# Edge weights kept in FP32 through the building of a dense graph: one FP32 one-hot product per slot in place of three BF16 products

## The chip, the core and the metric

The kernel runs on one core of a Trainium2 chip. The metric is device time in microseconds (us). Three runs of the kernel before took 4602.34, 4610.16 and 4604.41 us; the median is 4604.41.

The core has five engines that run side by side, each through its own list of instructions in order: TensorE (PE in the profile; its weight loads are PEld), VectorE (DVE), ScalarE (ACT), GpSimd (POOL) and SyncE (SP, which starts DMAs). SBUF is the on-chip memory of 128 partitions, PSUM the memory that TensorE writes its products to.

## The reference, cut to what matters

A graph of 3125 nodes (features of width 128) and 100,000 edges, sorted by target, goes through four layers, each of which normalises its input and adds its result to x. The change lies in how edges become matrices. Layer 0 (attention) and layer 2 need, for each pair of target and source node, how many edges join them. Layer 1 needs the sum of the edge weights of each pair:

```python
def spmv(v):
    return jax.ops.segment_sum(edge_vals[:, None] * v[edge_col], edge_row, num_segments=n)
...
edge_index = jnp.stack([src, dst])
h = jnp.maximum(_layernorm(x, axis=-1), 0.0)
x = x + _L0_gnn_ref(h, edge_index, ...)
h = jnp.maximum(_layernorm(x, axis=-1), 0.0)
x = x + _L1_gnn_ref(h, edge_weight, L1_gnn_weights, src, dst)
```

With the two dense matrices in hand, every sum over edges is a plain matrix product: counts (how many edges) is kept in SBUF as 8-bit floats, weights (the sum of edge weights) goes to device memory in FP32 and is read back in layer 1.

## The kernel before, in words

Nodes are cut into 25 blocks of 128 (NB). The edges of one target block and one source block go to a fixed number of slots of 128 edges each: CAP[db] slots for every source block, 8 for target block 0, 4, 3, 3 for the next three, 2 for blocks 4 to 18 and 1 for blocks 19 to 24. N_SLOTS is the number of slots of a target block, made even: 200, 100, 76, 76, then 50 and 26; 1358 in all, of which 1350 are used.

**Placing (place_edges, L924).** Edges lie in a tile of 112 rows by 896. VectorE works out the place of each edge in the table (the result is idx, L1056). Each edge has a record of 8 BF16 fields (FIELDS): its source within the block (SL), its target within the block (DL), three BF16 parts of its weight (WT to WT+2) and its type (TYPE). The three parts come from split3 (L913, called at L1060): ScalarE rounds the weight to BF16, VectorE subtracts, ScalarE rounds the rest, VectorE subtracts again; the three add up to the FP32 value. For each field TensorE turns the tile (L1074) and ScalarE writes it into rec (L1075), where neighbouring edges of one field lie 16 bytes apart. Then GpSimd issues 782 scatters (L1081), each of which writes 128 rows of 32 BF16 elements (ROOM, 64 bytes) to the table in device memory. ORDER puts the edges of target block 5 and up first, those of blocks 0 to 4 last.

**Building (build_block, L1137).** One call for each target block. SyncE loads the block's records into slots (L1151), once the scatters that hold its edges have landed. TensorE turns each field so that the 128 edges of a slot lie along the partitions (L1157); the result, keys, stays in PSUM, with one buffer. Then the slots go in batches of 8 (BATCH), of which there are 187. For each batch VectorE makes two one-hot matrices, oh_s and oh_d (L1174), which hold a 1 where the edge's source or target equals the column, and three products of oh_s with a part of the weight (L1176), together called oh_w. All are BF16 and lie in pairs of slots, so that the value of slot 2a+1 is next to that of slot 2a. For each slot TensorE adds one product of oh_s and oh_d to the counts (L1188) and three products of oh_d with the parts of oh_w to the weights (L1191). Both sums of two source blocks share one PSUM tile, ps_cw, with two buffers. When a pair is complete, ScalarE writes the counts to SBUF (L1195) and the weights to w_out (L1196), and after every second pair issues a DMA of w_out (L1199). At a block's end ScalarE checks in one instruction over 3200 elements that no count is above 15 (L1201, junk). The one-hots have two buffers each (b_hot).

**What sets the order.** GROUPS lists the target blocks: 5 to 8, 9 to 12, 13 to 16, 17 to 20, 21 to 24, then 0 to 2 and 3 to 4. Each group is built and then goes through the first attention (attend, L1318): 25 products u for each block (L1331, TensorE), then for each of 4 heads and 25 source blocks one masked count matrix on VectorE (over, L1340) and up to four products on TensorE (L1343). A scheduler sets the order of each engine's list before the run, by the order of the program and by when it reckons each instruction to be ready: so u products of a block stand between the slot products of the same group. After the last group come the second attention (to about 1840 us), layer 1, which reads the weights matrix three times, layer 2 and layer 3.

Of the kernel before, what the change touches and what calls it, by code (L numbers as in the profile page):

```python
# [18 lines left out]
P = 128  # L19
N = 3125  # L20
NB = 25
# [41 lines left out]
BATCH = 8  # L63
SL, DL, WT, TYPE = 0, 1, 2, 5
CB = [(q, min(4, NB - q)) for q in range(0, NB, 4)]


def bc(ap, shape):
    return ap.to_broadcast(shape)
# [829 lines left out]
class FastGnn(Gnn):  # L899
# [24 lines left out]
    def place_edges(self, placed):  # L924


        nc, tc, a = self.nc, self.tc, self.a
        self.table = self.dram.tile([TABLE, ROOM], BF16, name="table")
        self.types = self.dram.tile([1, EPART * EC], BF16, name="types")
# [4 lines left out]
        with ExitStack() as s:  # L934
# [6 lines left out]

            rec = placed.tile([P, EK * A * FIELDS + ROOM - FIELDS], BF16, name="rec")
            rec_of = rec[:, : EK * A * FIELDS].rearrange("p (k a f) -> p k a f", k=EK, f=FIELDS)
# [5 lines left out]
            for name, dt, fill, skip, queue in loads:  # L949
# [4 lines left out]
                queue.dma_start(t[whole:, : rest - skip], v[whole * EC + skip :][None, :])  # L954
            nc.gpsimd.memset(rec, 0.0)
            per = BASE[NB] // P
            none = work.tile([P, 14 * ROOM], BF16, name="none")
            nc.gpsimd.memset(none, -1.0)
            nc.sync.dma_start(self.table[: BASE[NB]].rearrange("(p i r) f -> p i (r f)", p=P, r=14),
                              bc(none[:, None, :], [P, per // 14, 14 * ROOM]))  # L960
            number = tile("number")
# [96 lines left out]
            w = raw["edge_weight"]  # L1058
            parts = [tile(f"w16_{i}", BF16) for i in range(3)]
            self.split3(parts, w, tile("rest"), V)  # L1060
            of_i = tile("of_i", I32)
            fields = [(WT + i, p) for i, p in enumerate(parts)]
            for f, name in ((SL, "src"), (DL, "dst")):
# [55 lines left out]
    def open_build(self, s, counts):  # L1119
# [13 lines left out]
        nc.vector.memset(self.minus_most, -MOST)  # L1133
        self.above = one.tile([P, NB], F32, name="above")
        self.junk = one.tile([P, NB, P], FP8, name="junk")

    def build_block(self, db):  # L1137
# [8 lines left out]

        keys = self.b_keys.tile([P, WT + 3, N_SLOTS[0]], BF16, name="keys")
        at = sum(N_SLOTS[:db])
        for a in range(halves):
            r = self.b_slots.tile([P, P, ROOM], BF16, name="slots")  # L1150
            ld = nc.sync.dma_start(r[:rows], self.table[BASE[db] + a * rows * P :][: rows * P].rearrange(  # L1151
                "(s e) f -> s e f", e=P))
# [13 lines left out]
        for x0 in range(0, n_slots, BATCH):  # L1166
            k = min(BATCH, n_slots - x0)
            h = k // 2
            wide = [P, h, P, 2]
            key = lambda f: bc(keys[:, f, x0 : x0 + 2 * h].rearrange("p (a b) -> p a b", b=2)[:, :, None, :], wide)  # L1170
            oh_s, oh_d = (self.b_hot.tile([P, BATCH // 2, P, 2], BF16, name=m) for m in ("oh_s", "oh_d"))
            oh_w = self.b_hot.tile([P, 3, BATCH // 2, P, 2], BF16, name="oh_w")
            for oh, f in ((oh_s, SL), (oh_d, DL)):
                nc.vector.tensor_tensor(oh[:, :h], bc(lane[:, None], wide), key(f), op=OP.is_equal)  # L1174
            for t in range(3):
                nc.vector.tensor_tensor(oh_w[:, t, :h], oh_s[:, :h], key(WT + t), op=OP.mult)  # L1176
            for x in range(k):
# [6 lines left out]
                if c == 0 and sb % 4 == 0:  # L1184
# [4 lines left out]
                                 skip_group_check=True)  # L1189
                for t in range(3):  # L1190
                    nc.tensor.matmul(ps[:, 1, j, :], lhsT=oh_d[of], rhs=oh_w[:, t][of], start=False,  # L1191
                                     stop=(last and t == 2), skip_group_check=True)
                if last and (j == 1 or sb == NB - 1):
# [7 lines left out]
        nc.scalar.activation(self.junk, self.counts[:, :, db * P : (db + 1) * P], AF.Relu, bias=self.minus_most,  # L1201
                             accum_out=self.above[:, db : db + 1], saturate=False)

# [690 lines left out]
```

## Time and profile before

| what | us |
|---|---|
| median of three runs | 4604.41 |
| the profiled execution's own time | 3488.11 |
| its span, first to last instruction | 3486.2 |
| first scatter of the placing starts | 139.63 |
| building and first attention, in turns | about 230 to 1325 |
| VectorE busy in all | 2391.4 (69%) |
| ScalarE busy in all | 663.7 (19%) |
| GpSimd scatters L1081 | 763.4, 782 of 976 ns |
| oh_s and oh_d, L1174 | 118.3 and 118.1 |
| oh_w, L1176 | 324.9, 561 of 631 ns |
| counts and weights products, L1188 and L1191 | 300.8 and 387.0 |
| drains, L1195 and L1196 | 122.7 and 117.5 |

The profiled execution is shorter than the median of the plain runs by 1116.3 us. The profile covers the profiled execution alone, and no view of it shows where the difference lies.

In a row of the profile the engine and the operation are followed by what is written and what is read, the shapes, and the number of instructions; then the busy time in us and the mean of one in ns; then the idle time just ahead of them and what ended it. In a timeline the first number is the start in us, the second how long the merged instructions took. Matmul records of TensorE overlap: the step from one start to the next tells the rate, not the length of one.

### The profile page before, as it was taken

Reading aid. Unit: us, or ns where it says so; the run is one execution under the profiler, and the core shown is the slowest. Engines: PE = TensorE matmul, PEld = TensorE weight load, DVE = VectorE, ACT = ScalarE, POOL = GpSimd, SP = SyncE. Lnnn points to the kernel's source line nnn. Section 1 sums busy time; section 2 is a strip of 40 time slices with the busy share of each in tenths; the row PEclk is TensorE's granted clock in tenths of the full one; section 3 lists DMA queues with packets and bytes.
Section 4 is the critical chain, followed back from the end, with each engine's and each line's share of the span. In section 5 each row is a group of like instructions: output and inputs, shape, how many; then the busy total and the mean of one; then the engine's idle time right before and its main releaser. Section 6 shows DMA issues by size and latency. Waiting matters only on the chain. (4 is left out here: it accounts for less than half of the span.)

```text
span 3486.2 us, 50781 instructions
## 1 busy us (share of the span) xinstructions
PE 2646.8 (76%) x20474; PEld 1841.3 (53%) x20474; DVE 2391.4 (69%) x3938; ACT 663.7 (19%) x1418; POOL 1286.3 (37%) x1305
## 2 busy tenths in 40 slices
PE   0146787878777887888885989796999957778886
PEld 0034465655556554555553444345555547777785
DVE  7976999999899998999994010214555565555665
ACT  1243041322501122000001000002021022222222
POOL 1377777777777000000000000001121017777775
PEclk9978999999999998999997999897999968999998
DMA  5012131211311110000003867660000033443432
GB/s 171 16 40 67 27 96 31 79 44 56 108 23 44 37 39 19 1 1 1 1 1 135 304 227 279 242 228 13 1 1 1 1 98 106 121 114 108 130 113 56
DMA packets 117351, 277.07 MB, mean 79 GB/s; under 512 B 28037, under 2 KB 67412, under 8 KB 106148
## 3 DMA queue, kind: packets, MB, share of 16 engines
q1 hardware_dynamic: 50566, 194.31, 16.3%
q0 software_dynamic: 40128, 37.42, 4.9%
q10 hardware_dynamic: 26412, 42.00, 3.4%
q8 instruction: 163, 2.67, 0.3%
q14 instruction: 82, 0.67, 0.1%
HBM read 210.66 MB, written 62.96 MB: 78 GB/s over the span
## 5 line engine op out<-in xcount | busy, mean ns | idle before, releaser
L1081 POOL DMA_INDIRECT table<-rec,idx x782 | 763.4, 976 | 368.1 <-issue 238.1
L1343 PE MATMUL ps_acc<-parts,over 128*128 128x198 bf16 x5000 | 622.7, 253 | 163.8 <-DVE over L1340 79.2
L1343 PEld LDWEIGHTS <-over 128*128 128x128 bf16 x5000 | 375.6, 98 | 407.8 <-DVE over L1340 384.2
L919 POOL TENSOR_TENSOR rest<-z,l_parts 128x640 f32<-128x640 f32 x15 | 21.0, 1400 | 1407.1 <-ACT l_parts L918 1407.1
L1778 POOL DMA_INDIRECT m_far<-pre,src_of x472 | 461.3, 977 | 193.4 <-issue 119.8
L1340 DVE SCALAR_TENSOR_TENSOR over<-ps_row,minus,counts 128x512 bf16<-128x512 f32 (+2 forms) x700 | 424.7, 685 | 9.2 <-PE ps_acc L1343 7.1
L1191 PE MATMUL ps_cw<-oh_w,oh_d 128*128 128x128 bf16 x4050 | 387.0, 225 | 53.3 <-DVE oh_w L1176 49.1
L531 PE MATMUL ps_sum<-g,v_node 128*128 128x512 f32 (+1 forms) x1050 | 403.7, 547 | 2.2 <-ACT v_node L482 2.2
L1340 DVE SCALAR_TENSOR_TENSOR over<-row,minus,counts 128x640 bf16<-128x640 f32 x500 | 401.9, 877 | 0.6 <-ACT row L1439 0.6
L1191 PEld LDWEIGHTS <-oh_d 128*128 128x128 bf16 x4050 | 306.0, 100 | 93.3 <-issue 71.8
L1188 PE MATMUL ps_cw<-oh_d,oh_s 128*128 128x128 bf16 x1350 | 300.8, 226 | 46.9 <-ACT w_out L1196 27.4
L1176 DVE TENSOR_TENSOR oh_w<-oh_s,keys 128x1024 bf16<-128x1024 bf16 (+2 forms) x561 | 324.9, 631 | 0.0
L1600 PE MATMUL ps_agg<-l_parts,counts 128*128 128x384 bf16 (+1 forms) x1875 | 313.6, 327 | 8.7 <-POOL l_parts L921 8.7
L531 PEld LDWEIGHTS ps_sum<-g,v_node 128*128 128x128 f32 x1050 | 188.0, 190 | 218.0 <-issue 215.2
L1483 DVE COPY v<-ps_sum 128x3200 f32<-128x3200 f32 x3 | 10.5, 3492 | 404.3 <-PE ps_sum L531 404.3
L1600 PEld LDWEIGHTS <-counts 128*128 128x128 fp8e4 x1875 | 183.2, 98 | 134.9 <-issue 9.6
L1799 PE MATMUL agg_far<-m_far,oh_far 128*128 128x128 f32 x1438 | 217.8, 303 | 47.7 <-ACT m_far L1785 43.4
L1799 PEld LDWEIGHTS agg_far<-m_far,oh_far 128*128 128x128 f32 x1438 | 195.9, 213 | 55.6 <-ACT m_far L1785 54.7
L1784 DVE TENSOR_TENSOR m_far<-ps_t,m_far 128x512 f32<-128x512 f32 x118 | 81.0, 688 | 165.9 <-DMA m_far<-pre,src_of 109.7
L1195 ACT ACTIVATE counts<-ps_cw 128x256 fp8e4<-128x256 f32 (+1 forms) x325 | 122.7, 378 | 333.4 <-PE ps_cw L1191 321.2
L1796 DVE TENSOR_TENSOR oh_far<-lane,keys 128x512 f32<-128x512 f32 (+3 forms) x194 | 124.1, 642 | 71.2 <-PE agg_far L1799 70.5
L1188 PEld LDWEIGHTS <-oh_s 128*128 128x128 bf16 x1350 | 134.4, 100 | 72.7 <-issue 46.3
(348 smaller groups left out, 3376.0 us busy)
## 6 DMA issues: line engine op xcount, KB each, us to landing
g<-weights SPq DMA_DIRECT2D x75, 1600.0 KB
weights<-w_out ACTq DMA_DIRECT2D x150, 256.0 KB
src_row<-wide SPq DMA_DIRECT2D x26, 512.0 KB
table<-rec,idx POOLq DMA_INDIRECT x782
type_row<-types SPq DMA_DIRECT2D x29, 384.0 KB
table<-none SPq DMA_DIRECT2D x1, 10864.0 KB
type_row<-wide SPq DMA_DIRECT2D x26, 384.0 KB
m_far<-pre,src_of POOLq DMA_INDIRECT x472
```

The lines of the kernel that those rows point to most:

```text
L531: nc.tensor.matmul(ps[:, c, :w], lhsT=y[:, b, :], rhs=flat[:, c0 : c0 + w], start=(b == 0), stop=(b == NB - 1))
L1081: st = nc.gpsimd.indirect_dma_start(out=self.table, out_offset=bass.IndirectOffsetOnAxis(ap=idx[:, k, p : p + 1], axis=0), in_=rec[:, (k * ...
L1176: nc.vector.tensor_tensor(oh_w[:, t, :h], oh_s[:, :h], key(WT + t), op=OP.mult)
L1188: nc.tensor.matmul(ps[:, 0, j, :], lhsT=oh_s[of], rhs=oh_d[of], start=(j == c == 0), stop=last, skip_group_check=True)
L1191: nc.tensor.matmul(ps[:, 1, j, :], lhsT=oh_d[of], rhs=oh_w[:, t][of], start=False, stop=(last and t == 2), skip_group_check=True)
L1195: nc.scalar.copy(self.counts[:, q : q + n, db * P : (db + 1) * P], ps[:, 0, :n], saturate=True)
L1340: V.scalar_tensor_tensor(over[:, : n * P], row, minus[:, sb, i : i + 1], self.counts[:, sb, cols], op0=OP.is_gt, op1=OP.mult)
L1343: nc.tensor.matmul(ps[:, j, : 3 * F2], lhsT=over[:, j * P : (j + 1) * P], rhs=parts[:, sb, i].rearrange("p s f -> p (s f)"), start=(sb == ...
L1600: nc.tensor.matmul(ps[:, :n], lhsT=self.counts[:, sb, db * P : (db + 1) * P], rhs=parts[:, sb, :n], start=(sb == 0), stop=(sb == NB - 1))
L1778: nc.gpsimd.indirect_dma_start(out=m[:, j, :], out_offset=None, in_=pre, in_offset=bass.IndirectOffsetOnAxis(ap=src_of[:, a + j : a + j + ...
L1796: V.tensor_tensor(oh[:, :r], bc(self.lane[:, None, :], [P, r, P]), bc(of[d][:, lo - LOW[d] : hi - LOW[d], None], [P, r, P]), op=OP.is_equal)
L1799: nc.tensor.matmul(agg[d], lhsT=oh[:, c - lo, :], rhs=m[:, c - a, :], start=(c == LOW[d]), stop=(c == ENDS[d] - 1))
```

## The change

The weight of an edge is kept as one FP32 word in its record, in the place of its first two BF16 parts; TYPE moves from field 5 to field 4. The record tile and the table become 32-bit words of the same number of bytes, and each scatter writes 16 words, 64 bytes as before. split3 is gone from the placing; the FP32 weights are turned by TensorE in two pieces and written into the records by ScalarE. In build_block, TensorE turns two BF16 fields and the FP32 weight. VectorE makes oh_s and oh_d as before and one FP32 product oh_w in place of three BF16 ones; ScalarE copies oh_d to FP32 (oh_d32). Both FP32 one-hots are written slot by slot, through a view in pairs. TensorE adds one FP32 product for each slot to the weights in place of three BF16 ones. The check of the counts is made in five pieces of 640 elements.

```diff
-SL, DL, WT, TYPE = 0, 1, 2, 5
+SL, DL, WT, TYPE = 0, 1, 2, 4
...
-        self.table = self.dram.tile([TABLE, ROOM], BF16, name="table")
+        self.table = self.dram.tile([TABLE, ROOM // 2], I32, name="table")
...
-            rec = placed.tile([P, EK * A * FIELDS + ROOM - FIELDS], BF16, name="rec")
+            words = placed.tile([P, (EK * A * FIELDS + ROOM - FIELDS) // 2], I32, name="rec")
+            rec = words.bitcast(BF16)
+            rec_w = words[:, : EK * A * FIELDS // 2].bitcast(F32).rearrange("p (k a f) -> p k a f", k=EK, f=FIELDS // 2)
...
-            nc.gpsimd.memset(rec, 0.0)
+            nc.gpsimd.memset(words, 0)
...
-            parts = [tile(f"w16_{i}", BF16) for i in range(3)]
-            self.split3(parts, w, tile("rest"), V)
+            for q, n in ((0, 4), (4, EK - 4)):
+                ps = psum2.tile([P, 4, A], F32, name="ps_idx")
+                for j in range(n):
+                    nc.tensor.transpose(ps[:, j, :], w[:, (q + j) * P : (q + j + 1) * P], self.ident[:A, :A])
+                nc.scalar.copy(rec_w[:, q : q + n, :, WT // 2], ps[:, :n])
             of_i = tile("of_i", I32)
-            fields = [(WT + i, p) for i, p in enumerate(parts)]
+            fields = []
...
-                    in_=rec[:, (k * A + p) * FIELDS :][:, :ROOM], in_offset=None)
+                    in_=words[:, (k * A + p) * FIELDS // 2 :][:, : ROOM // 2], in_offset=None)
...
-        self.junk = one.tile([P, NB, P], FP8, name="junk")
+        self.junk = one.tile([P, 5, P], FP8, name="junk")
...
-        keys = self.b_keys.tile([P, WT + 3, N_SLOTS[0]], BF16, name="keys")
+        both = self.b_keys.tile([P, 2, N_SLOTS[0]], F32, name="keys")
+        keys = both[:, 0].bitcast(BF16).rearrange("p (f x) -> p f x", f=2)
+        w_of = both[:, 1]
...
-            for f in range(WT + 3):
-                nc.tensor.transpose(keys[:, f, a * rows : (a + 1) * rows], r[:rows, :, f], self.ident16[:rows, :rows])
+            part = slice(a * rows, (a + 1) * rows)
+            for f in (SL, DL):
+                nc.tensor.transpose(keys[:, f, part], r[:rows, :, f], self.ident16[:rows, :rows])
+            nc.tensor.transpose(w_of[:, part], whole.bitcast(F32)[:rows, :, WT // 2], self.ident[:rows, :rows])
...
-            oh_w = self.b_hot.tile([P, 3, BATCH // 2, P, 2], BF16, name="oh_w")
+            oh_w, oh_d32 = (self.b_hot.tile([P, BATCH, P], F32, name=m) for m in ("oh_w", "oh_d32"))
+            paired = lambda t: t.rearrange("p (a b) n -> p a n b", b=2)[:, :h]
             for oh, f in ((oh_s, SL), (oh_d, DL)):
-                nc.vector.tensor_tensor(oh[:, :h], bc(lane[:, None], wide), key(f), op=OP.is_equal)
-            for t in range(3):
-                nc.vector.tensor_tensor(oh_w[:, t, :h], oh_s[:, :h], key(WT + t), op=OP.mult)
+                nc.vector.tensor_tensor(oh[:, :h], bc(lane[:, None], wide), key(keys[:, f]), op=OP.is_equal)
+            nc.vector.tensor_tensor(paired(oh_w), oh_s[:, :h], key(w_of), op=OP.mult)
+            nc.scalar.copy(paired(oh_d32), oh_d[:, :h])
...
-                for t in range(3):
-                    nc.tensor.matmul(ps[:, 1, j, :], lhsT=oh_d[of], rhs=oh_w[:, t][of], start=False,
-                                     stop=(last and t == 2), skip_group_check=True)
+                nc.tensor.matmul(ps[:, 1, j, :], lhsT=oh_d32[:, x, :], rhs=oh_w[:, x, :], start=False, stop=last,
+                                 skip_group_check=True)
...
-        nc.scalar.activation(self.junk, self.counts[:, :, db * P : (db + 1) * P], AF.Relu, bias=self.minus_most,
-                             accum_out=self.above[:, db : db + 1], saturate=False)
+        for q in range(0, NB, 5):
+            nc.scalar.activation(self.junk, self.counts[:, q : q + 5, db * P : (db + 1) * P], AF.Relu, bias=self.minus_most,
+                                 accum_out=self.above[:, db * 5 + q // 5 : db * 5 + q // 5 + 1], saturate=False)
```

More of the change, by code (lines that the diff above doesn't have):

```diff
@@ L959, in place_edges @@
             nc.sync.dma_start(self.table[: BASE[NB]].rearrange("(p i r) f -> p i (r f)", p=P, r=14),
-                              bc(none[:, None, :], [P, per // 14, 14 * ROOM]))
+                              bc(none.bitcast(I32)[:, None, :], [P, per // 14, 14 * ROOM // 2]))
             number = tile("number")
@@ L1133, in open_build @@
         nc.vector.memset(self.minus_most, -MOST)
-        self.above = one.tile([P, NB], F32, name="above")
-        self.junk = one.tile([P, NB, P], FP8, name="junk")
+        self.above = one.tile([P, NB * 5], F32, name="above")
+        self.junk = one.tile([P, 5, P], FP8, name="junk")
     def build_block(self, db):
@@ L1144, in build_block @@
         need = [self.placed[c] for c in range(LOW[db], ENDS[db])]
-        keys = self.b_keys.tile([P, WT + 3, N_SLOTS[0]], BF16, name="keys")
+        both = self.b_keys.tile([P, 2, N_SLOTS[0]], F32, name="keys")
+        keys = both[:, 0].bitcast(BF16).rearrange("p (f x) -> p f x", f=2)
+        w_of = both[:, 1]
         at = sum(N_SLOTS[:db])
         for a in range(halves):
-            r = self.b_slots.tile([P, P, ROOM], BF16, name="slots")
-            ld = nc.sync.dma_start(r[:rows], self.table[BASE[db] + a * rows * P :][: rows * P].rearrange(
+            whole = self.b_slots.tile([P, P, ROOM // 2], I32, name="slots")
+            r = whole.rearrange("p e f -> p (e f)").bitcast(BF16).rearrange("p (e f) -> p e f", f=ROOM)
+            ld = nc.sync.dma_start(whole[:rows], self.table[BASE[db] + a * rows * P :][: rows * P].rearrange(
                 "(s e) f -> s e f", e=P))
@@ L1169, in build_block @@
             wide = [P, h, P, 2]
-            key = lambda f: bc(keys[:, f, x0 : x0 + 2 * h].rearrange("p (a b) -> p a b", b=2)[:, :, None, :], wide)
+            key = lambda v: bc(v[:, x0 : x0 + 2 * h].rearrange("p (a b) -> p a b", b=2)[:, :, None, :], wide)
             oh_s, oh_d = (self.b_hot.tile([P, BATCH // 2, P, 2], BF16, name=m) for m in ("oh_s", "oh_d"))
-            oh_w = self.b_hot.tile([P, 3, BATCH // 2, P, 2], BF16, name="oh_w")
+            oh_w, oh_d32 = (self.b_hot.tile([P, BATCH, P], F32, name=m) for m in ("oh_w", "oh_d32"))
+            paired = lambda t: t.rearrange("p (a b) n -> p a n b", b=2)[:, :h]
             for oh, f in ((oh_s, SL), (oh_d, DL)):
-                nc.vector.tensor_tensor(oh[:, :h], bc(lane[:, None], wide), key(f), op=OP.is_equal)
-            for t in range(3):
-                nc.vector.tensor_tensor(oh_w[:, t, :h], oh_s[:, :h], key(WT + t), op=OP.mult)
+                nc.vector.tensor_tensor(oh[:, :h], bc(lane[:, None], wide), key(keys[:, f]), op=OP.is_equal)
+            nc.vector.tensor_tensor(paired(oh_w), oh_s[:, :h], key(w_of), op=OP.mult)
+            nc.scalar.copy(paired(oh_d32), oh_d[:, :h])
             for x in range(k):
```

## The prediction, made before the changed kernel ran

> **What bounds the kernel now.** I read the page's slices first, then busy time by windows, then the groups by line, and last the timeline of single engines inside one block. Only two stages hold lines that the change touches: the placing of the edges (0 to 140 us) and the building of the blocks (230 to 1285 us), which alternates with the attention of each group.
>
> ```profile
> DVE  7976999999899998999994010214555565555665
> ACT  1243041322501122000001000002021022222222
> ...
> 400.00:500.00 100.00, 82.62 (x934) 62.67 (x935) 95.61 (x168) 38.96 (x100) 76.20 (x79) 0.97 0.26 77
> 1000.00:1100.00 100.00, 73.89 (x911) 59.18 (x910) 95.05 (x159) 12.81 (x33) 76.22 (x79) 0.93 0.11 28
> ```
>
> Slices 4 to 16 (87 us each) show VectorE at 9 and ScalarE at 1 to 3. The windows (PE, PEld, DVE, ACT, POOL busy, clock) say the same of two building stretches: VectorE 95%, ScalarE 13 to 39%, clock 0.93 to 0.97. So VectorE paces the builds.
>
> ```profile
> L1191 PE MATMUL ps_cw<-oh_w,oh_d 128*128 128x128 bf16 x4050 | 387.0, 225 | 53.3 <-DVE oh_w L1176 49.1
> L1176 DVE TENSOR_TENSOR oh_w<-oh_s,keys 128x1024 bf16<-128x1024 bf16 (+2 forms) x561 | 324.9, 631 | 0.0
> L1331 PE MATMUL ps_u<-parts,counts 128*128 128x396 bf16 x625 | 149.3, 354 | 9.2 <-ACT counts L1195 7.9 <-DVE u L1333 0.4
> L1201 ACT ACTIVATE junk<-counts,minus_most 128x3200 fp8e4<-128x3200 fp8e4 x25 | 74.1, 2966 | 0.0
> L1749 DVE TENSOR_TENSOR oh_wide<-lane,keys 128x512 f32<-128x512 f32 (+1 forms) x113 | 76.6, 678 | 18.1 <-PE agg_wide L1761 17.7 <-ACT keys L1735 0.3
> L1075 ACT COPY rec<-ps_rec 128x784 bf16<-128x784 bf16 x6 | 21.4, 3823 | 0.0
> ```
>
> TensorE's weight products wait for VectorE's oh_w, and oh_w waits for nothing (0.0). L1749 and L1075 are my prices for an FP32 VectorE product and for a strided ScalarE write.
>
> ```profile
> 256.24 0.68 DVE L1174 TENSOR_TENSOR oh_s<-lane,keys 128x1024 bf16<-128x1024 bf16 x1
> 256.83 0.68 DVE L1174 TENSOR_TENSOR oh_d<-lane,keys 128x1024 bf16<-128x1024 bf16 x1
> 257.43 1.88 DVE L1176 TENSOR_TENSOR oh_w<-oh_s,keys 128x1024 bf16<-128x1024 bf16 x3
> 259.23 0.68 DVE L1174 TENSOR_TENSOR oh_s<-lane,keys 128x1024 bf16<-128x1024 bf16 x1
> ...
> 430.54 0.22 PE L1188 MATMUL ps_cw<-oh_d,oh_s 128*128 128x128 bf16 x1
> 430.59 0.33 PE L1191 MATMUL ps_cw<-oh_w,oh_d 128*128 128x128 bf16 x3
> 430.77 0.22 PE L1188 MATMUL ps_cw<-oh_d,oh_s 128*128 128x128 bf16 x1
> ...
> 3186.43 0.22 PE L1756 MATMUL ps_m<-type,type_hot 96*128 96x128 bf16 x1
> 3186.43 0.97 PEld L1799 LDWEIGHTS agg_far<-m_far,oh_far 128*128 128x128 f32 x8
> 3186.49 1.11 PE L1799 MATMUL agg_far<-m_far,oh_far 128*128 128x128 f32 x8
> ...
> 128.12 10.65 ACT L1075 COPY rec<-ps_rec 128x784 bf16<-128x784 bf16 x3
> 138.58 1.59 ACT L1114 CAST in_order<-ps_idx 128x448 int32<-128x448 f32 x2
> ```
>
> A batch of 8 slots takes VectorE 2.99 us (256.24 to 259.23), that is 5 steps of 0.598. TensorE needs 0.228 us for a slot's four BF16 products (430.54 to 430.77), 1.82 us a batch. An FP32 product leaves two records: L1799 has 1438 records for 719 products. Eight such records follow one BF16 product; a record is 0.275 us long (median of L1799), so the last starts at 3187.33, eight steps of 0.112 us after the BF16 start at 3186.43. The BF16 product's own step is thus also 0.112, not 0.057: the FP32 weight load behind it is longer.
>
> **The skill.** "TensorE: Matmul & The Clock Gate", Weight-path perf modes, says that the fast weight load brings nothing for FP32; the 0.112 us step agrees. "VectorE: DVE Perf Modes", the perf-mode tier table, gives tensor_tensor twice the rate in BF16 only; 631 ns for 1024 BF16 elements against 678 for 512 FP32 agree. "ScalarE: Activation LUTs", What ACT_TABLE_LOAD costs, gives 186 ns plus 0.833 ns an element. "SBUF — State Buffer", Specifications, says that each move to another 16-byte line pays a penalty, without a price. L1075 writes 2-byte elements 16 bytes apart at 4.9 ns each (3823/784), L1114 FP32-sized ones 28 bytes apart at about 2.0 (1.59 us for 784), so the trace agrees.
>
> **The change part by part.** The sum is made against the profiled execution: 3488.11 us, its span of 3486.2 and 1.9 around it. The median of the runs is 1116.3 us above that, and no view shows where; I carry this part over unchanged.
>
> Placing: split3 loses two VectorE instructions of 1.07 us and two casts beside it; three rec copies of 3.6 us go, and two FP32 ones come, which need only the loaded weights and can run in ScalarE's idle time from 45 to 117 us. Now the rec copies end at 138.8 us and the first scatter starts at 139.6. Then idx, ready at 137.9 now and 2.1 earlier, is what is late. Gain 3.5 us (between 0 and 5). The scatters keep their number and 64-byte rows. Memset, fill and loads lie in the wait for inputs or move the same bytes: nothing.
>
> VectorE: per batch two one-hots at 0.598 and one FP32 product. From L1749, 0.678 plus 512 more elements at 0.96 GHz gives 1.21 us long, a step of 1.13. The batch is 2.33 in place of 2.99. Over 1358/8 = 170 full batches that frees 112 us, if nothing else binds. The product writes FP32 to places 512 bytes apart in turn; no VectorE row shows such a write. Floor 1.13, ceiling 2.2 (two cycles an element); I take the floor, since the copy below is the longer of the two either way.
>
> TensorE: a slot becomes one BF16 product and two FP32 passes in alternation, 3 x 0.111 = 0.333 us; 2.66 a batch. The u products (L1331) run in the same stage: 25 per block at 0.17 us, 0.68 a batch of a 50-slot block. So 3.34, above VectorE's old 2.99. A block's key transposes drop from five to three: under 0.3 us a block, nothing.
>
> ScalarE: the drains of a pair (L1195, L1196) take 0.61 us back to back, 1.3 a batch with the DMA issue. The new copy reads 1024 elements and writes FP32 alternately to two places 512 bytes apart. Floor 1.04 us (the ScalarE page's formula), ceiling 5.0 (L1075's 4.9 ns); I take 1.9, near L1114, the nearest write of the same width. The check of counts in five pieces costs 3.9 us a block for 2.97. ScalarE is thus 3.8 us busy per batch of a 50-slot block.
>
> The new wait: the FP32 product waits for the copy; behind it on TensorE stand all later slots and u, and VectorE waits for them to free its buffers. Each one-hot has two buffers and PSUM two pairs, so batch n+1 follows the end of batch n-1 by two one-hots (1.25), the copy (1.9), the drain that frees PSUM (0.65), then its own 3.34: 7.14 for two, 3.57 a batch. A 50-slot block takes 6.25 x 3.57 = 22.3, plus 2.1 at its start (keys 0.4, first product 3.2 late, 1.5 filled by u): 24.4 for the 20.8 measured between the starts of blocks at 444.8 and 465.6 us. Twelve such blocks are not held by scatters: +43. Six blocks of 26 slots: ScalarE's 8.6 drains, 3.9 check and 6.3 copies make 18.8 for 14.0 or less: +4.5 each, +27. Four wide blocks: (1.25 + 1.9 + 2.83)/2 = 3.0 a batch, as now, +4 at starts. With the placing: 43 + 27 + 4 - 3.5 = +70.5. The attention stages between, the second attention and layers 1 to 3 don't change. Profile 3559, median 4675.
>
> **The rivals.** A, not slower: VectorE's saving reaches the end. If the copy costs at most 1.05 us and the u products slip into the attention stage, where VectorE paces, a batch needs TensorE's 2.66: 0.33 x 170 = 56 us less, 4548. For it: VectorE's 95% and ScalarE's idle 60%. Against: u runs between the products today. It decides from the point at which a batch falls below 2.99.
>
> B: the copy is cheap, TensorE binds with u inside. 50-slot blocks +1.3 x 12, small ones +2 x 6 (ScalarE's check and drains), wide ones -0.16 x 56, placing -3.5: +15, 4619. For it: the formula; against: L1114.
>
> C: ScalarE serves the drains of batch n before the copy for n+1, or the copy costs near 5 us. Serialised, a batch is 3.34 + 0.65 + 1.9 less the hidden counts, 5.5: 2.5 x 75, plus 34 for small and 115 for wide blocks: +337, 4941. For it: the drains stand earlier in the program; against: u at 427.88 shows that the order follows readiness, and the copy is ready first.
>
> **How the numbers follow.** Forecast 0.47, its own range 4630 to 4735 (copy 1.3 to 2.7 us). A 0.18, B 0.22, C 0.13. B straddles: 0.02 faster, 0.09 within 0.2% (about what a measurement can tell from none), 0.11 slower. Faster 0.20, same 0.09, slower 0.71. From 4530 to 4760 holds the forecast, B and most of A; C and the lowest of A, under 0.2, stay out. If the 1116 us is a slower TensorE, the loss grows; if it is slower scatters, they hold the builds and it shrinks.
>
> **What would show it.** The copy's mean (1.9), block starts 24 us apart in place of 20.8, TensorE 0.333 a slot, VectorE idle in builds behind TensorE, first scatter near 136 us. A copy near 1.05 with VectorE still above 90% would prove the forecast wrong.

## The result and the profile after

The changed kernel takes 4734.68 us (median of 4 runs, 4733.06 to 4742.38), the kernel before 4607.28 in the runs beside it. The ratio is 1.0276, with a 95% interval from 1.0254 to 1.0299: slower, by some 127 us.

The first profile of the kernel before took 3488.11 us, which none of its plain runs did (4584 to 4635 us in all). A second profile of the same kernel (the first run of the experiments) took 4613.69 us, like the plain runs. The two profiles compared from here on are that one and the profile of the changed kernel (4734.26 us, span 4732.5). First the page of the changed kernel: the slices of VectorE and ScalarE (118 us each), then groups.

```profile
DVE  8502000000488788797889998011145463444545
ACT  0101000000434634646420001000021111121222
...
L1201 PE MATMUL ps_cw<-oh_w,oh_d 128*128 128x128 f32 x2700 | 538.8, 331 | 113.1 <-ACT oh_d L1187 89.2
...
L1187 ACT CAST oh_d<-oh_d 128x1024 f32<-128x1024 bf16 (+2 forms) x187 | 337.6, 1845 | 395.6 <-DVE oh_d L1185 393.8
...
L1186 DVE TENSOR_TENSOR oh_w<-oh_s,keys 128x1024 f32<-128x1024 bf16 (+2 forms) x187 | 335.8, 1796 | 50.2 <-remote 50.2
```

The same slices (115 us each) and the old products on the page of the second profile of before:

```profile
DVE  8502000000299999999899993101345563344444
ACT  0201000000113322211300001000011121122221
...
L1191 PE MATMUL ps_cw<-oh_w,oh_d 128*128 128x128 bf16 x4050 | 398.5, 227 | 95.8 <-DVE oh_w L1176 50.6
...
L1176 DVE TENSOR_TENSOR oh_w<-oh_s,keys 128x1024 bf16<-128x1024 bf16 (+2 forms) x561 | 324.8, 630 | 0.0
```

Three things are to be seen. In both of these profiles VectorE does next to nothing in slices 5 to 10: the builds run only after the last scatter (its end is at 1206.1 us before, 1204.7 after). By the end of the second attention (2780.1 us, against 1840.8 in the first profile) this makes 939 of the 1116 us that the first profile lacked; the rest lies in the layers behind it. Then, in the builds, VectorE falls from 9s to mostly 7s and 8s, and ScalarE rises from between 1 and 3 to between 3 and 6. And the oh_w products cost VectorE 335.8 us, more than the 324.8 of the three BF16 ones that they replace.

The windows show who paces now. The columns are the stretch and its length in us, busy time and instructions of PE, PEld, DVE, ACT and POOL, then PE's clock, DMA share and GB/s. In the second profile of before: a piece of the scatters, then the stretch between two attentions that builds blocks 10 to 12.

```profile
900.00:1140.00 240.00, 13.47 (x84) 8.52 (x84) 7.24 (x15) 6.08 (x12) 184.19 (x172) 0.50 0.05 10
...
1385.00:1447.00 62.00, 53.37 (x669) 42.62 (x669) 59.17 (x110) 33.27 (x84) 0.00 (x0) 1.00 0.30 101
```

The same two stretches of the changed kernel:

```profile
900.00:1140.00 240.00, 21.02 (x85) 15.34 (x85) 13.47 (x13) 12.46 (x23) 184.40 (x172) 0.50 0.05 10
...
1395.00:1487.00 92.00, 78.38 (x580) 65.62 (x580) 65.50 (x76) 74.02 (x140) 0.00 (x0) 0.93 0.20 71
```

Those three blocks took 62 us with VectorE busy 95% of it; now they take 92 with TensorE at 85%, ScalarE at 80% and VectorE at 71%. No engine is full: they hand work to each other and wait. One wait, in ScalarE's timeline of the changed kernel (start, length in us):

```profile
1587.42 0.83 ACT L1212 ACTIVATE junk<-counts,minus_most 128x640 fp8e4<-128x640 fp8e4 x1
...
1588.37 0.83 ACT L1212 ACTIVATE junk<-counts,minus_most 128x640 fp8e4<-128x640 fp8e4 x1
...
1589.20 3.76 ACT L1187 CAST oh_d<-oh_d 128x1024 f32<-128x1024 bf16 x2
...
1596.92 0.38 ACT L1205 ACTIVATE counts<-ps_cw 128x256 fp8e4<-128x256 f32 x1 [0.99 <-PE ps_cw L1201]
1597.20 0.37 ACT L1206 COPY w_out<-ps_cw 128x256 f32<-128x256 f32 x1
1597.45 2.02 ACT L1187 CAST oh_d<-oh_d 128x1024 f32<-128x1024 bf16 x1
```

VectorE's timeline of the same kernel says when those copies could have begun:

```profile
1586.52 0.68 DVE L1185 TENSOR_TENSOR oh_d<-lane,keys 128x1024 bf16<-128x1024 bf16 x1
...
1595.36 0.68 DVE L1185 TENSOR_TENSOR oh_d<-lane,keys 128x1024 bf16<-128x1024 bf16 x1
```

And TensorE's timeline what it costs:

```profile
1588.12 0.22 PE L1199 MATMUL ps_cw<-oh_d,oh_s 128*128 128x128 bf16 x1
1591.21 0.49 PE L1201 MATMUL ps_cw<-oh_w,oh_d 128*128 128x128 f32 x2 [2.87 <-ACT oh_d L1187]
...
1593.12 0.31 PE L1199 MATMUL ps_cw<-oh_d,oh_s 128*128 128x128 bf16 x1
...
1593.76 0.31 PE L1199 MATMUL ps_cw<-oh_d,oh_s 128*128 128x128 bf16 x1
```

The oh_d that ends at 1587.20 is copied from 1589.20 on: ScalarE first finishes pieces of the check of the block before. The oh_d that ends at 1596.04 is copied from 1597.45 on: in ScalarE's list the drain of the batch ahead stands first, and it waits for TensorE. From the end of an oh_d to the start of its copy it is 1.50 us in the mean (123 copies between 1230 and 2100 us). TensorE waits 2.87 us for the first copy, and soon after takes 0.64 us a slot (1593.12 to 1593.76) in place of 0.333. The windows around it show the granted clock of TensorE, the third number from the end:

```profile
1591.20:1592.35 1.15, 1.14 (x10) 1.11 (x11) 1.15 (x2) 1.15 (x1) 0.00 (x0) 1.00 0.00 0
1592.35:1595.75 3.40, 3.40 (x19) 3.09 (x18) 1.07 (x3) 1.70 (x5) 0.00 (x0) 0.50 0.02 5
1595.77:1600.00 4.23, 3.86 (x32) 3.11 (x31) 4.18 (x5) 3.24 (x7) 0.00 (x0) 1.00 0.17 64
```

The slots of 0.64 us are those at half clock. Between the last scatter and the last product of the builds TensorE is busy at half clock for 113 us in the changed kernel and for 49 us in the second profile of before.

### The profile page after: what moved, and what is told of

Same layout as the page of the kernel before. It is cut to its first block, busy times and chain, and to the rows that moved or that the text cites. A ratio compares the mean times of both kernels' runs of the same rounds, so it can differ in the third digit from the quotient of the medians.

```text
span 4732.5 us, 48211 instructions
## 1 busy us (share of the span) xinstructions
PE 2862.1 (60%) x19058; PEld 2033.6 (43%) x19058; DVE 2403.3 (51%) x3562; ACT 994.4 (21%) x1802; POOL 1340.9 (28%) x1305
## 5 line engine op out<-in xcount | busy, mean ns | idle before, releaser
L1086 POOL DMA_INDIRECT table<-rec,idx x782 | 816.8, 1045 | 380.8 <-issue 250.6
L1201 PE MATMUL ps_cw<-oh_w,oh_d 128*128 128x128 f32 x2700 | 538.8, 331 | 113.1 <-ACT oh_d L1187 89.2
L1199 PE MATMUL ps_cw<-oh_d,oh_s 128*128 128x128 bf16 x1350 | 315.6, 235 | 475.9 <-remote 310.2
L1201 PEld LDWEIGHTS ps_cw<-oh_w,oh_d 128*128 128x128 f32 x2700 | 461.0, 216 | 181.9 <-ACT oh_d L1187 119.6
L1185 DVE TENSOR_TENSOR oh_s<-lane,keys 128x1024 bf16<-128x1024 bf16 (+2 forms) x187 | 118.7, 635 | 796.8 <-remote 648.9
L1187 ACT CAST oh_d<-oh_d 128x1024 f32<-128x1024 bf16 (+2 forms) x187 | 337.6, 1845 | 395.6 <-DVE oh_d L1185 393.8
L1186 DVE TENSOR_TENSOR oh_w<-oh_s,keys 128x1024 f32<-128x1024 bf16 (+2 forms) x187 | 335.8, 1796 | 50.2 <-remote 50.2
L1342 PE MATMUL ps_u<-parts,counts 128*128 128x396 bf16 x625 | 165.2, 362 | 191.8 <-remote 109.4
L1772 PE MATMUL agg_wide<-m_wide,oh_wide 128*128 128x128 f32 x900 | 157.6, 329 | 163.4 <-ACT m_wide L1769 123.6
L1342 PEld LDWEIGHTS <-counts 128*128 128x128 fp8e4 x1250 | 120.5, 101 | 290.7 <-issue 168.7
```

The lines of the kernel that those rows point to most:

```text
L1086: st = nc.gpsimd.indirect_dma_start(out=self.table, out_offset=bass.IndirectOffsetOnAxis(ap=idx[:, k, p : p + 1], axis=0), in_=words[:, (k ...
L1186: nc.vector.tensor_tensor(paired(oh_w), oh_s[:, :h], key(w_of), op=OP.mult)
L1187: nc.scalar.copy(paired(oh_d32), oh_d[:, :h])
L1199: nc.tensor.matmul(ps[:, 0, j, :], lhsT=oh_s[of], rhs=oh_d[of], start=(j == c == 0), stop=last, skip_group_check=True)
L1201: nc.tensor.matmul(ps[:, 1, j, :], lhsT=oh_d32[:, x, :], rhs=oh_w[:, x, :], start=False, stop=last, skip_group_check=True)
L1342: nc.tensor.matmul(wide[:, : HEADS * 3 * F1], lhsT=self.counts[:, sb, (a + q) * P : (a + q + 1) * P], rhs=parts[:, sb, :, :, F1:], start=( ...
```

## The experiments

Ratios are to runs of the kernel before on the same chip (medians 4614.96, 4601.48 and 4609.35 us in the three groups of four).

**The kernel before, profiled again.** No edit.

> The kernel before, unchanged, to see a profile of it in the condition of its plain runs (about 4605 us). Theory S: the 1116 us that its plain runs have above its first profile is a stall of all engines beside the scatters: as in the profile of the changed kernel, between about 163 and 1200 us TensorE, VectorE and ScalarE advance by about one instruction per scatter (some 1.3 us), TensorE under 15 % and VectorE under 10 % busy there, and the builds run only after the last scatter, from about 1200 to 2300 us. Then building and first attention after the scatters take some 1110 us here, against 1238 in the changed kernel (1200 to 2438). Rival: the stall belongs to the change (its 32-bit table or the new copies). Then this profile shows builds beside the scatters, VectorE above 85 % from 230 us on, and the missing 1100 us lie elsewhere, e.g. in slower products in layers 1 to 3.

Measured: 4613.69 us. The stall is there without the change, as its lines above show; the rival falls. From the last scatter to the second attention it is 1098 us (1206.1 to 2303.7), in the changed kernel 1232 (1204.7 to 2437.1). The last oh_d of the builds ends at 2216.2 us, in the changed kernel at 2348.5: the whole loss is made by then (+132), and nothing is added later.

**Both FP32 one-hots in pairs, or one of them.** Both writers then write in one run, and TensorE reads with a step of 8 bytes:

```diff
-            oh_w, oh_d32 = (self.b_hot.tile([P, BATCH, P], F32, name=m) for m in ("oh_w", "oh_d32"))
+            oh_w, oh_d32 = (self.b_hot.tile([P, BATCH // 2, P, 2], F32, name=m) for m in ("oh_w", "oh_d32"))
...
-            nc.vector.tensor_tensor(paired(oh_w), oh_s[:, :h], key(w_of), op=OP.mult)
-            nc.scalar.copy(paired(oh_d32), oh_d[:, :h])
+            nc.vector.tensor_tensor(oh_w[:, :h], oh_s[:, :h], key(w_of), op=OP.mult)
+            nc.scalar.copy(oh_d32[:, :h], oh_d[:, :h])
...
-                nc.tensor.matmul(ps[:, 1, j, :], lhsT=oh_d32[:, x, :], rhs=oh_w[:, x, :], start=False, stop=last,
+                nc.tensor.matmul(ps[:, 1, j, :], lhsT=oh_d32[of], rhs=oh_w[of], start=False, stop=last,
```

Both: 

> Both FP32 one-hots lie in pairs of slots like the BF16 ones, so that VectorE and ScalarE write them in one run; TensorE then reads each FP32 one-hot with a step of two elements (8 bytes). Theory W (the strided write costs both writers): oh_w falls from 1796 to about 1210 ns, the copy from 1845 to about 1050 ns; a 50-slot block's start to start falls from 28.5 to about 23 us, the whole from 4735 to about 4640 (between 4600 and 4680). Rival R (TensorE's FP32 products, 0.333 us a slot with the counts, bind whatever the writers cost): 4720 to 4740, the writers shorter but idle longer. Rival P (the step of two slows TensorE's FP32 reads): the step of 0.112 us a pass grows, the products' records go above 331 ns, and the time is 4735 or more.

Only oh_w: 

> Only VectorE's product oh_w lies in pairs (written in one run, read by TensorE with a step of two); the copy oh_d32 still goes to two places in turn. Theory W: oh_w about 1210 ns, the copy stays near 1845; since TensorE waits for the copy (the page names it for 89.2 us before the products), little comes of it: 4700 to 4735. Rival V (VectorE's three instructions are what paces a batch): most of the gain of both paired comes already here, 4640 to 4670. Rival X (the two writers slow each other): the copy shortens too, below 1700.

Only the copy: 

> Only ScalarE's copy oh_d32 lies in pairs; oh_w is still written to two places in turn. Theory W: the copy about 1050 ns, oh_w stays near 1796; the wait of TensorE on the copy shrinks by 0.8 us a batch: 4650 to 4690, more than half of what both paired give. Rival V (VectorE paces): 4715 to 4735. Rival X (the writers slow each other): oh_w shortens too, below 1650.

| one-hots in pairs | oh_w, ns | copy, ns | ratio (95% interval) | median, us |
|---|---|---|---|---|
| none (the change) | 1796 | 1845 | 1.0276 (1.0254 to 1.0299) | 4734.68 |
| oh_w | 1117 | 1846 | 1.0263 (1.0213 to 1.0314) | 4742.20 |
| copy | 1804 | 972 | 1.0112 (1.0075 to 1.0149) | 4668.16 |
| both | 1116 | 972 | 1.0120 (1.0069 to 1.0172) | 4671.09 |

From the groups of the kernel with only the copy in pairs:

```profile
L1202 PE MATMUL ps_cw<-oh_w,oh_d 128*128 128x128 f32 x2700 | 532.6, 327 | 67.0 <-ACT oh_d L1188 36.4
...
L1187 DVE TENSOR_TENSOR oh_w<-oh_s,keys 128x1024 f32<-128x1024 bf16 (+2 forms) x187 | 337.4, 1804 | 50.3 <-remote 50.3
...
L1188 ACT CAST oh_d<-oh_d 128x1024 f32<-128x1024 bf16 (+2 forms) x187 | 179.3, 972 | 411.5 <-DVE oh_d L1186 409.1
```

Theory W holds on the durations: each writer's time depends on its own layout alone, so they don't slow each other (rival X falls, and rival R with the time). But only the copy is on the path: TensorE's wait for it falls from 89.2 to 36.4 us, and 1.6% of the 2.8% is gone, some 76 us; 0.68 us less on VectorE for each oh_w gives nothing that can be told. Rival V falls with it. Of the loss 1.1% stays, some 52 us. The copy alone gives all that both give; with only oh_w in pairs the time is a little above theory W's range, and with both it is above the 4640 named, though in the range; a 50-slot block takes 26.4 us then (1556.8 to 1583.2), not some 23. Rival P holds in part: TensorE's records keep their 331 ns, but at full clock the median step from slot to slot is 0.347 us with both in pairs, 0.345 with the copy alone and 0.339 with oh_w alone, against 0.333. The copy in pairs (alone) also lessens the half clock: TensorE is busy at it for 76 us in the builds, in place of 113. How much of the 76 us gained comes by that way was not separated.

**The copy earlier in the program.** The one-hots of a batch and its copy are written ahead of the products of the batch before:

```diff
-        for x0 in range(0, n_slots, BATCH):
+        def make(x0):
...
+            return k, h, oh_s, oh_d, oh_w, oh_d32
+
+        made = make(0)
+        for x0 in range(0, n_slots, BATCH):
+            k, h, oh_s, oh_d, oh_w, oh_d32 = made
+            if x0 + BATCH < n_slots:
+                made = make(x0 + BATCH)
```

With the layout of the change: 

> The changed kernel with one reordering of the program: the one-hots of a batch and their copy are written before the products of the batch ahead of it, so that in ScalarE's list each copy stands before that batch's drains; both writes stay in two places in turn. Theory O (in the changed kernel the copy of every second batch stands in ScalarE's list behind the drains of the batch ahead, and the first one of a block behind pieces of the check, so TensorE idles for the copy): TensorE's idle time ahead of the FP32 products on the copy falls from 89 us to below 40, a 50-slot block from 28.5 to 23 to 25 us, the whole from 4735 to 4660 to 4690. Rival B (the two buffers of each one-hot alone set the cadence, 3.57 us a batch, as the prediction's recurrence has it, and the order in the list does not matter): 4720 to 4740.

With the copy in pairs: 

> The same reordering with the copy in pairs of slots (972 ns instead of 1845). Theory T (what is left then is TensorE's own work, 0.333 us a slot plus 25 u products, some 22 us a 50-slot block against 20.8 before): 4620 to 4645, a 50-slot block at 22 to 23 us. Rival B (buffers): no better than the paired copy alone, 4660 to 4675. Rival O alone (all of the loss is the place of the copy in the list): 4600 to 4620, no slower than before.

Batches of 4, four buffers, copy in pairs: 

> The one before with batches of 4 slots and four buffers of each one-hot in the room of two of 8. If the granularity of two buffers of 8 slots still holds TensorE back, this falls below it by 10 us or more; if TensorE's own work binds (theory T), it is within 10 us of it; if the fixed cost of each VectorE and ScalarE instruction (twice as many) decides, it is 15 us or more above it.

The first takes 4700.67 us, ratio 1.0220 (1.0192 to 1.0249): 0.56% less than the change, some 26 us, between the two theories. From the end of oh_d to its copy it is now 0.72 us in the mean, and TensorE's wait for the copy 57.5 us, where below 40 had been expected. So the place in ScalarE's list is a part of the loss, but, as far as this order removes it, the smaller one. With the copy in pairs the reordering gives nothing: 4666.04 us, 1.0152 (1.0116 to 1.0187), and batches of 4 neither: 4671.95 us, 1.0152 (1.0120 to 1.0184). My 4620 to 4645 for the second was wrong: the time is that of rival B. Its reason, the buffers, is not shown. Four buffers of half the size hold as many slots as two, so that run tests finer pieces and not more room. Against B speaks the window of blocks 10 to 12 in the second kernel, with TensorE at 92%:

```profile
1383.00:1458.00 75.00, 69.31 (x547) 60.23 (x547) 63.80 (x72) 55.44 (x131) 0.00 (x0) 0.98 0.24 83
```

TensorE is nearly full there, and its 69.3 us alone are more than the 62 that VectorE needed before. I had put a slot at 0.333 us, but with the paired copy it takes 0.345 (median of the steps from one counts product to the next, between 1340 and 2200 us), and the stretch holds u products too.

**One BF16 product in place of the FP32 one.** Starting from both in pairs, TensorE takes the upper 16 bits of each word:

```diff
+                high = lambda t: t.rearrange("p a n b -> p (a n b)").bitcast(BF16).rearrange("p (a n b) -> p a n b", n=P, b=4)[:, x // 2, :, 2 * (x % 2) + 1]
...
-                nc.tensor.matmul(ps[:, 1, j, :], lhsT=oh_d32[of], rhs=oh_w[of], start=False, stop=last,
+                nc.tensor.matmul(ps[:, 1, j, :], lhsT=high(oh_d32), rhs=high(oh_w), start=False, stop=last,
```

> Both FP32 one-hots in pairs, written as before, but TensorE reads only the upper 16 bits of each word as BF16, so that a slot's weight product is one BF16 product; the weights matrix then holds weights cut to BF16. Copy, oh_w, waits and buffers are those of the kernel with both paired (4671). Theory T (TensorE's FP32 passes carry what the paired layout leaves): 4671 falls by 50 us or more, to 4560 to 4620, VectorE's 2.4 us a batch or the copy being what is left. Rival O (the place of the copy in ScalarE's list carries it): 4645 to 4675, with TensorE idle in place of busy.

Then also without the copy:

```diff
-            nc.scalar.copy(oh_d32[:, :h], oh_d[:, :h])
...
-                nc.tensor.matmul(ps[:, 1, j, :], lhsT=high(oh_d32), rhs=high(oh_w), start=False, stop=last,
+                nc.tensor.matmul(ps[:, 1, j, :], lhsT=oh_d[of], rhs=high(oh_w), start=False, stop=last,
```

> The kernel with both one-hots paired and the upper halves read as BF16 (4551), without the copy: the weight product takes oh_d itself and the upper half of oh_w, so the weights matrix holds weights cut to BF16. Theory A (VectorE's shorter batch, 0.598 + 0.598 + 1.07 = 2.27 us, reaches the end once TensorE has neither FP32 passes nor a wait for the copy): about 150 batches run after the last scatter, 0.72 us less for each against the kernel before: 4485 to 4515. Rival K (the copy is hidden there already, and something else, the drains and u products, holds a block at some 20 us): 4535 to 4555.

The first takes 4550.71 us, 0.9895 (0.9872 to 0.9919): 2.25% below both in pairs, some 104 us, with the same copy and buffers. TensorE's wait for the copy is even longer (88.7 us in place of 38.1) and its clock lower (0.88 in the window below). Theory T holds, and the time is even below its range: the FP32 passes carry more than what the paired layout left. The second takes 4488.81 us, 0.9747 (0.9709 to 0.9785), in theory A's range. The window of blocks 10 to 12 in each, first with the copy:

```profile
1351.00:1425.00 74.00, 56.90 (x428) 37.61 (x428) 52.68 (x75) 55.93 (x133) 0.00 (x0) 0.88 0.27 92
```

and without it:

```profile
1348.00:1405.00 57.00, 50.66 (x428) 39.17 (x427) 53.24 (x78) 39.18 (x115) 0.00 (x0) 0.91 0.37 122
```

With the copy no engine is above 77%; without it VectorE paces again, at 93%. So the hand-over from VectorE over ScalarE to TensorE costs up to 1.5% even with a copy of 978 ns, where TensorE has time to wait. It is "up to" because the second kernel also reads oh_d 4 bytes apart where the first reads the copy's halves 8 bytes apart: at full clock the median slot goes from 0.179 to 0.176 us, the fastest tenth from 0.174 to 0.155. These two kernels are faster than the kernel before and the changed one, but not in the same arithmetic.

**The kernel before with fewer oh_w instructions.** Its third weight part left out in the builds, in VectorE's product and in TensorE's:

```diff
-            for t in range(3):
+            for t in range(2):
                 nc.vector.tensor_tensor(oh_w[:, t, :h], oh_s[:, :h], key(WT + t), op=OP.mult)
...
-                for t in range(3):
+                for t in range(2):
                     nc.tensor.matmul(ps[:, 1, j, :], lhsT=oh_d[of], rhs=oh_w[:, t][of], start=False,
-                                     stop=(last and t == 2), skip_group_check=True)
+                                     stop=(last and t == 1), skip_group_check=True)
```

> The kernel before with the third weight part left out in the builds (two oh_w products and two weight products a slot). It tests the first claim, that VectorE paces the builds of the kernel before: 0.598 us less a batch on about 150 batches after the scatters, 80 to 95 us less than before (4510 to 4525). If TensorE, ScalarE or the buffers pace them, under 40 us less.

Measured: 4515.07 us, 0.9786 (0.9742 to 0.9830), 94 us less. One instruction of 0.598 us less a batch would be worth 0.55 us on each of 170 batches. But TensorE has a product less too (a slot of 0.173 us in place of 0.230, 0.46 a batch), so this run alone doesn't tell the two apart. Two other numbers do. Blocks 10 to 12 take 51 us in place of 62, again with VectorE at 95%:

```profile
1366.00:1417.00 51.00, 45.38 (x528) 34.83 (x526) 48.25 (x89) 33.09 (x86) 0.00 (x0) 1.00 0.37 122
```

And the kernel without the copy has nearly the same slot on TensorE (0.176 us) and 0.12 us less a batch on VectorE (2.27 against 2.39): it is faster again, by 26 us, where 170 times 0.12 are 20. VectorE did pace the builds before.

**Two BF16 parts in one word.** From the kernel before: parts 1 and 2 lie side by side in the record, one FP32 product makes both one-hots, and TensorE reads the halves. The third part is left out of the builds:

```diff
-            for t in range(3):
-                nc.vector.tensor_tensor(oh_w[:, t, :h], oh_s[:, :h], key(WT + t), op=OP.mult)
+            nc.vector.tensor_tensor(oh_w[:, :h], oh_s[:, :h], key(w_of), op=OP.mult)
...
+                    nc.tensor.matmul(ps[:, 1, j, :], lhsT=oh_d[of], rhs=of_w[:, x // 2, :, 2 * (x % 2) + 1 - t], start=False,
```

> The kernel before with the first two BF16 parts of a weight kept side by side as one 32-bit word: one FP32 product on VectorE makes both (a word times 1 or 0 keeps its bits), TensorE reads its halves as two BF16 products; the third part, the last 8 bits of the weight, is left out. VectorE 2.27 us a batch, TensorE 1.37 plus u. Theory A: 4490 to 4520, within 15 us of the one without copy. Rival: reading halves 8 bytes apart slows TensorE's weight products, above 4540.

With the third part as before: 

> The same with the third part as a BF16 product of its own, so that nothing of the weight is left out: VectorE 3 x 0.598 + 1.07 = 2.86 us a batch against 2.99. Theory A: 0.13 us on about 150 batches, 15 to 25 us less than before (4580 to 4590). Rival: the FP32 product does not overlap with its neighbours as BF16 ones do, and nothing is left of the gain (within 5 us of before).

Both missed theory A. The first takes 4604.94 us, 0.9995 (0.9976 to 1.0013), the second 4702.23 us, 1.0203 (1.0171 to 1.0234). VectorE has what was planned (oh_w 1116 ns), but TensorE does not. The weight products of the first:

```profile
L1196 PE MATMUL ps_cw<-oh_w,oh_d 128*128 128x128 bf16 x2700 | 417.5, 291 | 26.4 <-DVE oh_w L1180 25.5
```

and of the kernel with two parts left, with the same number of products but a step of 4 bytes in place of 8:

```profile
L1191 PE MATMUL ps_cw<-oh_w,oh_d 128*128 128x128 bf16 x2700 | 307.5, 232 | 42.2 <-DVE oh_w L1176 36.2
```

At full clock a slot of one counts and two weight products takes 0.293 us in the first and 0.173 here (medians). With the third part a slot takes 0.350 us, against 0.230 in the kernel before. The rival named for the first of the two holds: halves 8 bytes apart cost TensorE what VectorE saved. The second, 93 us above the kernel before, lies outside what either theory had named for it. I found no version that keeps the whole weight and beats the kernel before.

## Why the prediction was right, and where not

The direction held, and so did its main reason: TensorE's FP32 passes and a copy that TensorE waits for cost more than VectorE can bring. That VectorE's batch would get shorter did not hold. The loss was put at 70.5 us and is some 127.

- **The range.** Here luck helped. 4734.68 lies at the top end of the forecast's own range (4630 to 4735), and those ends stood for a copy of 1.3 and of 2.7 us. The copy came out at 1.85, next to the 1.9 from which 4675 was worked out. So the term that set the range is not what filled it.
- **VectorE paces the builds before.** Shown by its 95% of the windows and by the kernel with two weight parts (94 us), taken with the one without the copy. (ScalarE's slices 4 to 16 run from 0 to 5, not from 1 to 3 as read; nothing hangs on it.)
- **The 1116 us carried over unchanged.** Right in effect. Most of them are a stall beside the scatters, which both kernels have. Neither guess on them held. The builds come after the stall, so the loss didn't shrink; and that twelve 50-slot blocks (7 to 18), the number taken, lie behind the last scatter is luck, since the number came from a profile without the stall.
- **Placing.** The first scatter starts at 137.0 us, near the 136 forecast; of the 2.8 us gained, 1.4 are left at the last scatter. The two FP32 copies did not run in ScalarE's idle time but last of all, from 135.1 to 136.7 us.
- **The copy.** 1845 ns in the mean (2010 for a full batch) for the 1.9 taken. "SBUF — State Buffer", Specifications, gave a penalty without a price; the two layouts differ by 873 ns for the mean copy, though no run shows that it is this penalty. In pairs a full batch takes 1049 ns (by shape, in the kernel with only the copy in pairs), as "ScalarE: Activation LUTs", What ACT_TABLE_LOAD costs, has it: an estimate of 186 + 1024 x 0.833 = 1039.
- **VectorE's FP32 product.** The floor was the wrong end of the bracket: a full batch takes 1963 ns long in two places in turn against 1215 in pairs (1.21 had been worked out without the layout). So VectorE saves nothing. For the time it doesn't matter here, as argued: shortening oh_w alone changed nothing that can be told.
- **TensorE.** 0.333 us a slot, as forecast, in the median step. But the forecast priced every slot at full clock: of 959 steps between 1340 and 2200 us, 85 lie wholly at half clock, where the median is 0.640.
- **The sum by blocks, the term that was mis-sized.** Taking the starts of the keys in both profiles, the twelve 50-slot blocks lost 80.5 us (from -9.7 at block 7 to +70.8 at block 19), 6.7 each where 3.6 were forecast; the six of 26 slots lost 37.4, 6.2 each where 4.5 were (by the forecast's own numbers, 18.8 less 14.0, it should have said 4.8); the wide blocks and block 4 lost 24.1 where 4 were. These are 142.0; less the 9.7 us by which the changed kernel starts block 7 earlier they make the 132.
- **A 50-slot block** takes 28.5 us (TensorE's timeline, the starts of two blocks' keys) where 24.4 were forecast. In the changed kernel:

```profile
1395.63 0.25 PE L1166 MATMUL keys<-ident,slots 50*128 50x50 bf16 x2
...
1424.12 0.25 PE L1166 MATMUL keys<-ident,slots 50*128 50x50 bf16 x2
```

and in the second profile of before, 20.8 as in the first:

```profile
1384.70 0.29 PE L1157 MATMUL keys<-ident,slots 50*128 50x50 bf16 x2
...
1405.49 0.31 PE L1157 MATMUL keys<-ident,slots 50*128 50x50 bf16 x2
```

- **The step that failed**, in size, is the recurrence of 7.14 us for two batches. It starts the copy as soon as oh_d is there and lets everything else overlap. The trace shows 1.50 us between the two in the mean: the copies stand in a fixed list behind drains and pieces of the check. The order behind rival C was given little weight because "the order follows readiness"; reordering the program gave back some 26 of the 57 us of excess. The largest candidate for the rest is TensorE's half clock, for which the recurrence has no term: half of the 64 us more that TensorE is busy at it, some 32 us, is an estimate of what it costs. Waits and half clock go together in these runs (76 us of it with the copy in pairs, 98 with the reordering), and no run changes the clock alone, so the shares stay open.
- **Rivals.** A named its own condition, that TensorE doesn't bind and the copy is cheap; where both were made true, VectorE's saving did reach the end (4488.81 us). B describes the kernel with the copy in pairs (TensorE busy for 91% of the time of blocks 10 to 12), but at 4668, not 4619. Of these 49 us some 16 are the slower slot (0.012 us times 1350) and some 14 the half clock (half of 76 less 49), both estimates; the rest is open. C's full price of 5.5 us a batch did not come: 28.5 us for a 50-slot block are 28.5/6.25 = 4.6 a batch.

## What to carry to other kernels

Before work is moved off the engine that paces, add up what the next engine does per batch in the same stretch; here TensorE's FP32 passes left no room for the gain. A value made by one engine, converted by a second and read by a third pays for its place in the second one's list, not only for its duration: look at the time from ready to start, and not only at the mean length. A forecast for TensorE that waits now and then needs a term for its granted clock. And look at both ends of a layout: writing to two places in turn made the FP32 writes 1.6 and 1.9 times as long (1963 ns against 1215, 2010 against 1049), and a read with a step of 8 bytes can cost the reader what the writer saved.

## What the hardware did that was not expected

While the scatters run, engines wait tens of us after the work that they need has ended. All thirteen profiles taken after the first one show it, whatever the kernel; the first profile of before, which lacks it, shows that it need not be so. ("remote" in brackets is a source that the profile can't name.) In the second profile of before, TensorE has done the products of a whole batch by 454.55 us and then waits itself. ScalarE's first drain, which needs a part of them, comes at 488.61:

```profile
488.61 0.38 ACT L1195 ACTIVATE counts<-ps_cw 128x256 fp8e4<-128x256 f32 x1 [45.66 <-remote]
```

VectorE, in the same kernel, then waits for its buffers:

```profile
452.69 1.88 DVE L1176 TENSOR_TENSOR oh_w<-oh_s,keys 128x1024 bf16<-128x1024 bf16 x3
516.61 0.69 DVE L1174 TENSOR_TENSOR oh_s<-lane,keys 128x1024 bf16<-128x1024 bf16 x1 [62.05 <-remote]
```

What delays them was not tested. It ends with the last scatter. In the first profile the scatters kept nearly the same pace (139.6 to 1141.1 us, against 139.8 to 1206.1) and the builds ran beside them.

TensorE reads one-hots 8 bytes apart more slowly than one-hots 4 bytes apart, but only at full clock. There a slot with an FP32 copy 8 bytes apart takes 0.345 us against 0.333, and a slot of three BF16 products, of which two read halves 8 bytes apart, 0.293 against 0.173. At half clock the same pairs of kernels take 0.640 and 0.640, 0.320 and 0.320 (medians, between 1340 and 2200 us): the step costs nothing there. So half the clock makes the slot of three dense products 1.85 times as long and the one with the stepped halves only 1.09 times.
